# The first layer of a four-layer graph network: program order on three engines, edge sums of two adjacency blocks together, node sums by transposes, an earlier u and later weights

## The chip, the cores and the metric

The kernel runs on one core of one Trainium2 chip. The metric is the device time of one execution in microseconds (us). Every execution also has a mean granted clock of the tensor engine.

PE is the tensor engine, DVE the vector engine, ACT the scalar engine, SP the engine that issues most loads. PEld is PE loading weights.

## The reference, cut to what matters

Four layers follow each other, each a residual and a layer norm around a graph layer on the same 4096 x 4096 adjacency matrix. The change touches only layer 0.

```python
def _L0_gnn_ref(h, node_adj, edge_adj, W, a):      # both matrices are adj
    hw = h @ W
    pos = (node_adj > 0).astype(hw.dtype)
    neg = (node_adj < 0).astype(hw.dtype)
    h_plus, h_minus = pos @ hw, neg @ hw
    a1, a2 = (a[:F_OUT], a[F_OUT:])
    e_plus = leaky_relu((h_plus @ a1 + h_minus @ a2)[:, 0], ALPHA)
    ...
    scores = jnp.where(edge_adj > 0, e_plus[None, :], NEG_INF)
    scores = jnp.where(edge_adj < 0, e_minus[None, :], scores)
    attn = softmax(scores, axis=1)
    return attn * edge_adj @ hw

x = _layernorm(x + _L0_gnn_ref(x, adj, adj, W, a))
...                                                 # three more layers
```

The matrix has no negative entry with these inputs (the kernel checks it and has a slow path for it), so the layer needs two things: for every node the sum of u = hw @ a1 over its edges, from which e follows, and then products of the matrix with hw scaled by exp(e), with their normaliser.

## The kernel before

The matrix is cut into 8 x 8 blocks of 512 x 512, one load of 1 MB each. The **first pass** runs over the eight rows of blocks. In each block DVE makes a mask of the edges, PE sums u over the edges, and ACT looks for negative entries. At the end of row i the sums are copied (the tile `parts`), and e, its exponential and the scaled hw of row i follow. Products with blocks whose hw is already scaled are done at once. Up to two blocks behind the diagonal are kept on the chip and used later; the **second pass** loads the others again.

```python
def masks(a):
    pos = l0w.tile([P, TB, IB], BF16, name="pos", bufs=4)
    nc.vector.tensor_scalar(pos, a, 0.0, None, op0=ALU.is_gt)
    return pos

def edge_sums(pe, pos, j, wgt, first, last):
    for k in range(TB):
        nc.tensor.matmul(pe[32 * k:32 * k + 32, :], wgt[:, j * TB + k, :], pos[:, k, :], start=first, stop=last)

def columns(parts):                       # node sums: four products with two columns
    pc = ps_tr.tile([P, TB, 2], F32, name="ptr")
    for k in range(TB):
        nc.tensor.matmul(pc[:, k, :], parts[:, k * P:(k + 1) * P], sel, start=True, stop=True)
    return pc

for i in range(NB):                       # first pass
    ...
    for n, j in enumerate(order):
        a = chunk(l0k if i < j <= i + 2 else ld, adjT, i, j)            # (shortened)
        pos = masks(a)
        edge_sums(pe, pos, j, both, n == 0, n == NB - 1)
        nc.scalar.activation(junk, a, AF.Relu, scale=-1.0, accum_out=...)
        if n == 1 and rest:
            diagonal(*rest)               # of row i - 1
            if i >= 3:
                above(i - 3, kept.pop(i - 3))
        ...
        while n > 0 and known:
            j, a = known.pop(0)
            product(p, j, a, j == 0, False)
    if i == 4:
        tc.keep_in_program_order(nc.sync.dma_start(x, ...))             # 2 MB
    nc.scalar.copy(parts, pe)
    sums = columns(parts)
    ...                                   # e, Exp, hw scaled, split into three bf16 parts
```

The framework that builds the kernel chooses the order of instructions on each engine itself; the text of the program only says what depends on what.

The softmax here doesn't subtract the row's maximum and nothing guards it: scores larger than these inputs give would overflow.

## Time and profile before

| | kernel before |
|---|---|
| median of 3 runs | 2280.73 us (2279.25 to 2281.05) |
| span of the profiled run | 2278.0 us |
| busy | PE 96%, DVE 52%, ACT 26% |
| sums of rows 0, 3 and 7 complete | 51.1, 123.9, 265.3 us |
| first product of layer 1 | 353.5 us |

A line of the timeline reads: start, duration, engine, source line, operation, what is written from what is read, shapes, number of instructions in a row, and in brackets how long the engine had been idle and who released it. The start of a row in the kernel before (row 5, PE):

```profile
189.49 0.95 PE L341 MATMUL ptr<-sel,parts 128*128 128x2 f32 x8
190.30 1.10 PE L346 MATMUL pacc<-keep,hw 128*128 128x512 f32 x2
191.33 0.40 PE L334 MATMUL pden<-pos,both 128*32 128x512 bf16 x4
192.02 0.40 PE L334 MATMUL pmm<-pos,xp 128*32 128x512 bf16 x4 [0.29 <-DVE pos L328]
193.83 3.70 PE L346 MATMUL pacc<-chunk,hw 128*128 128x512 f32 x8 [1.41 <-DVE hw L411]
```

Each f32 matmul shows as two records, called passes below, so the product with one block, four matmuls, is eight passes. The `x8` at 189.49 are the node sums. While DVE works on e behind them, PE does two passes of a kept block and edge sums, and is idle for 0.29 + 1.41 us. The product behind runs at full clock: eight passes in 3.70 us.

### The profile page before, as it was taken

To read this page: it belongs to the slowest core of one execution; us is meant where nothing else is said; L and a number is where in the kernel's file an instruction comes from. 1 tells how busy PE (TensorE), PEld (TensorE's weight loads), DVE (VectorE), ACT (ScalarE), POOL (GpSimd) and SP (SyncE) were. 2 spreads that over 40 slices of the span, in tenths; PEclk is the share of its full clock that TensorE was granted. 3 is DMA by queue.
4 is the path that set the end of the run, shared out by engine and by line. 5 is a ranking of instruction groups with operands and counts; after the bars stand their busy time and mean duration, and the time that the engine had idled before them with its cause. 6 is when DMAs were issued, how large, how long until landed. Compare 5 with 4: busy or idle time off the path is not lost.

```text
span 2278.0 us, 22715 instructions
## 1 busy us (share of the span) xinstructions
PE 2176.3 (96%) x8552; PEld 843.0 (37%) x8552; DVE 1176.9 (52%) x1709; ACT 593.6 (26%) x1012; POOL 836.9 (37%) x540
## 2 busy tenths in 40 slices
PE   4899999999999999999999999879999999999998
PEld 3333444444444444444443333212222322232233
DVE  4554462000010110000026777779999999999955
ACT  4764200000000000000032222334444443443320
POOL 0000000000000000000004555669999999999930
PEclk9899999999999999999999999999999999999999
DMA  7886658889777677778876556434666666666665
GB/s 279 336 334 232 213 178 273 300 299 302 266 256 242 233 263 242 263 266 271 274 245 230 201 186 220 167 111 149 223 254 241 224 244 243 243 234 238 238 226 203
DMA packets 83608, 549.14 MB, mean 241 GB/s; under 512 B 9376, under 2 KB 15520, under 8 KB 17568
## 3 DMA queue, kind: packets, MB, share of 16 engines
q1 hardware_dynamic: 75200, 542.15, 68.1%
q10 hardware_dynamic: 8288, 5.44, 0.8%
q8 instruction: 69, 1.13, 0.2%
q14 instruction: 51, 0.42, 0.1%
HBM read 545.46 MB, written 2.10 MB: 240 GB/s over the span
## 4 chain that ended last, share of the span: by engine, by line
PE 83%; DVE 10%; issue 3%; ACT 2%; DMA 1%; ACTq 0%; POOL 0%; DVEq 0%; POOLq 0%
PE pacc L514 29%; PE pacc L346 10%; PE den L705 9%; PE pp L769 9%; PE pp L861 8%; PE num L705 7%; DVE tau L688 5%; DVE tau L691 2%; PE pmm L540 2%; PE num L769 1%; PE pden L334 1%; PE num L861 1%; PE px L135 1%; PE ptr L135 1%; ACT a L666 1%
## 5 line engine op out<-in xcount | busy, mean ns | idle before, releaser
L688 DVE SCALAR_TENSOR_TENSOR tau<-D,es,a 128x1024 f32<-128x1024 f32 x512 | 630.7, 1273 | 27.7 <-ACT a L666 27.5
L693 POOL TENSOR_TENSOR tau<-tau,chunk 128x1024 f32<-128x1024 f32 x256 | 609.4, 2380 | 16.7 <-DVE tau L688 15.9
L612 POOL TENSOR_TENSOR x<-x,B2R 128x512 f32<-128x512 f32 x8 | 10.2, 1279 | 1176.3 <-PE px L135 1176.3
L705 PE MATMUL den<-tau,cs 128*32 128x512 f32 x2048 | 357.0, 608 | 30.7 <-DVE tau L688 22.9
L666 ACT ACTIVATE a<-chunk 128x1024 f32<-128x1024 f32 x232 | 238.7, 1029 | 453.3 <-DVE tau L691 387.6
L705 PE MATMUL num<-tau,hc 128*32 128x512 f32 x2048 | 346.5, 600 | 0.6 <-POOL tau L693 0.6
L692 POOL TENSOR_TENSOR tau<-tau,chunk 128x320 f32<-128x320 f32 x256 | 222.8, 870 | 155.6 <-DVE tau L688 106.2
L769 PE MATMUL pp<-chunk,xT 128*128 128x512 f32 x448 | 236.1, 629 | 0.0
L691 DVE TENSOR_TENSOR tau<-tau,a 128x704 f32<-128x704 f32 x256 | 225.4, 881 | 0.0
L514 PE MATMUL pacc<-chunk,t 128*128 128x512 f32 x512 | 223.5, 592 | 0.0
L514 PE MATMUL pacc<-chunk,v 128*128 128x512 f32 x512 | 222.5, 592 | 0.0
L514 PE MATMUL pacc<-chunk,x 128*128 128x512 f32 x512 | 221.9, 592 | 0.0
L861 PE MATMUL pp<-chunk,w 128*128 128x512 f32 x448 | 208.1, 602 | 2.4 <-ACT xT L565 1.6
L346 PE MATMUL pacc<-chunk,hw 128*128 128x512 f32 x408 | 196.7, 622 | 2.3 <-DVE hw L411 2.3
L705 PEld LDWEIGHTS den<-tau,cs 128*32 128x32 f32 x2048 | 57.9, 107 | 270.2 <-DVE tau L688 180.1
L705 PEld LDWEIGHTS num<-tau,hc 128*32 128x32 f32 x2048 | 88.7, 110 | 145.0 <-issue 132.3
L514 PEld LDWEIGHTS pacc<-chunk,v 128*128 128x128 f32 x512 | 97.2, 190 | 122.0 <-issue 122.0
L514 PEld LDWEIGHTS pacc<-chunk,x 128*128 128x128 f32 x512 | 96.4, 190 | 116.7 <-issue 116.7
L514 PEld LDWEIGHTS pacc<-chunk,t 128*128 128x128 f32 x512 | 96.1, 190 | 115.3 <-issue 115.3
L769 PEld LDWEIGHTS pp<-chunk,xT 128*128 128x128 f32 x448 | 71.7, 188 | 158.6 <-issue 144.3
L561 DVE COPY w<-ptr 128x512 f32<-128x512 f32 x8 | 5.5, 691 | 241.5 <-PE ptr L135 241.5
L861 PEld LDWEIGHTS pp<-chunk,w 128*128 128x128 f32 x448 | 80.5, 190 | 115.7 <-issue 111.6
(190 smaller groups left out, 1443.5 us busy)
## 6 DMA issues: line engine op xcount, KB each, us to landing
chunk<-in_adjT SPq DMA_DIRECT2D x386, 1024.0 KB, 4.9
chunk<-in_adj SPq DMA_DIRECT2D x116, 1024.0 KB, 4.9
keep<-in_adjT SPq DMA_DIRECT2D x13, 1024.0 KB, 6.9
xT<-in_xT ACTq DMA_DIRECT2D x8, 256.0 KB, 6.1
out<-o ACTq DMA_DIRECT2D x8, 256.0 KB, 5.1
W1A<-in_w1a ACTq DMA_DIRECT2D x1, 384.0 KB, 5.6
W1B<-in_w1b ACTq DMA_DIRECT2D x1, 384.0 KB, 6.4
W0T<-in_w0gT ACTq DMA_DIRECT2D x1, 64.0 KB, 5.6
```

The source lines that it names most:

```text
L135: nc.tensor.transpose(p[:, k, :], src(k), ident)
L346: nc.tensor.matmul(p, hw[:, j * TB + k, :], a[:, k, :], start=first and k == 0, stop=last and k == TB - 1)
L514: nc.tensor.matmul(p, stationary(c * TB + k), a[:, k, :], start=n == 0 and k == 0, stop=n == NB - 1 and k == TB - 1)
L540: nc.tensor.matmul(ph, W1A[:, k, hh * P:(hh + 1) * P], r, start=k == 0, stop=k == 2)
L666: nc.scalar.activation(ap, a, AF.Copy, accum_out=deg[:, nt, self.mp:self.mp + 1])
L688: nc.vector.scalar_tensor_tensor(tau[:, h, :], self.D[:, h].rearrange("p b i -> p (b i)"), es[:, nt, 2 * self.hp + h:2 * self.hp + h + 1], ap,
L691: nc.vector.tensor_tensor(tau2[:, 0, 0:OWN], tau[:, 0, 0:OWN], ap[:, 0:OWN], ALU.mult)
L692: nc.gpsimd.tensor_tensor(tau2[:, 0, OWN:WB], tau[:, 0, OWN:WB], a[:, OWN:WB], ALU.mult)
L693: nc.gpsimd.tensor_tensor(tau2[:, 1, :], tau[:, 1, :], a, ALU.mult)
L705: nc.tensor.matmul(acc[q:q + 32, :], weights(nt, 2 * self.hp + h, is_den), r[:, h, mb * IB:(mb + 1) * IB], start=nt == 0, stop=nt == NT - 1)
L769: nc.tensor.matmul(p, y[:, (2 * mp + c) * TB + k, :], a[:, k, :], start=c == 0 and k == 0, stop=c == 1 and k == TB - 1)
L861: nc.tensor.matmul(p, w[:, c * TB + k, :], a[:, k, :], start=c == 0 and k == 0, stop=c == NB - 1 and k == TB - 1)
```

## The change

The intent: let PE, DVE and ACT run in an order written by hand, so that edge sums of two blocks stand together (fewer switches between bf16 and f32 on PE), node sums come from transposes and a vector sum instead of products with two columns, u = x @ (W a) is made first so that the masks can start early, and weights of later layers are loaded when they are not in the way. The core of the diff, with cuts marked:

```diff
-    for g in range(NB):
-        nc.scalar.dma_start(xT[:, g * IB:(g + 1) * IB], xT_in[:, g * IB:(g + 1) * IB])
+    for g in range(2):
+        half = slice(g * N // 2, (g + 1) * N // 2)
+        nc.sync.dma_start(xT[:, half], xT_in[:, half])
...                                        (later weights: collected in `loads`)
+            manual.enter_context(tc.manual_schedule(engines={mybir.EngineType.PE, mybir.EngineType.DVE,
+                                                             mybir.EngineType.Activation}))
+            WA = l0.tile([P, 2], F32, name="WA")
...
+                for k in range(NT // 2):
+                    t = half * NT // 2 + k
+                    nc.tensor.matmul(pu[:, k, :], xT[:, t * P:(t + 1) * P], WA, start=True, stop=True)
...
-                pos = l0w.tile([P, TB, IB], BF16, name="pos", bufs=4)
+                pos = l0w.tile([P, TB, IB], BF16, name="pos", bufs=6)
...
-            def columns(parts):
...
+            def column(dst, q, col):
+                nc.vector.tensor_reduce(dst, q.rearrange("p k (g c) -> p k g c", g=4)[:, :, :, 3 * col:3 * col + 3],
+                                        AX.XY, ALU.add)
...
             for i in range(NB):
...
                     pos = masks(a)
-                    edge_sums(pe, pos, j, both, n == 0, n == NB - 1)
+                    sums.append((j, pos))
+                    if j < i:
+                        known.append((j, a))
+                    if n == 0 and diag:
+                        if behind:
+                            product(diag.p, *behind[0], behind[0][0] == 0, False)
+                        scores(i - 1, parts)
+                        for b in behind[1:]:
+                            product(diag.p, *b, False, False)
+                    if n == 2 and i >= 3:
+                        above = Above(i - 3)
...
+                    elif n % 2:
+                        for m, (b, ps) in enumerate(sums):
+                            edge_sums(pe, ps, b, both, n == 1 and m == 0, False)
+                        sums = []
+                        then = (diag if n == 1 else above if n == 3 else None)
+                        if then:
+                            then.sums()
+                            then.products()
+                            ends.append(then.store)
...
+                        while len(known) > int(n == NB - 3):
+                            b = known.pop(0)
+                            product(p, *b, b[0] == 0, False)
+                    if (i, n) == (1, 3):
+                        for t, src in loads:
+                            tc.keep_in_program_order(nc.sync.dma_start(t, src))
...                                        (second pass: blocks in pairs, loaded and masked one pair ahead)
+                then = Above(NB - 3) if n == 1 else Above(NB - 2) if n == 3 else None
+                if n + 1 < len(pairs):
+                    ahead = load(*pairs[n + 1])
+                while ends:
+                    ends.popleft()()
```

`while len(known) > int(n == NB - 3)` is the held-back product: one block's product waits for the start of the next row, so that PE has something to do while `parts` is copied and transposed.

## The prediction

> **What bounds the kernel now.** I read the page first, then the busy time of every engine stretch by stretch, then the timeline of single instructions in the first 360 us, then the waits of the DMA queue. The page's slices say that after a short ramp the tensor engine never rests:
>
> ```profile
> PE   4899999999999999999999999879999999999998
> ...
> DVE  4554462000010110000026777779999999999955
> ACT  4764200000000000000032222334444443443320
> ...
> PEclk9899999999999999999999999999999999999999
> ```
>
> Each digit is 57 us. Only the first slices are under 9 on PE, and only there is the granted clock below 0.9. The change touches the first layer alone. Layer 1 begins with its first product at 353.5 us (first start of the group of line 514 that reads x), so the first layer owns 353 of 2278 us, and everything behind it is moved as a block. What the change is worth is therefore how far that start moves. The same view by engine in five stretches of that layer:
>
> ```profile
> core 0: us, PE busy (x) PEld busy (x) DVE busy (x) ACT busy (x) POOL busy (x), PEclk, DMA share, GB/s
> 0.00:50.00 50.00, 19.69 (x95) 14.87 (x99) 22.06 (x92) 21.68 (x33) 0.70 (x6) 0.99 0.81 303
> 50.00:95.00 45.00, 38.57 (x148) 15.33 (x140) 22.86 (x38) 35.11 (x41) 0.00 (x0) 0.78 0.90 365
> 95.00:124.00 29.00, 26.66 (x95) 10.29 (x96) 14.78 (x23) 17.55 (x21) 0.00 (x0) 0.88 0.69 266
> 124.00:265.00 141.00, 139.05 (x478) 56.10 (x481) 62.39 (x94) 70.54 (x80) 0.00 (x0) 1.00 0.73 253
> 265.00:353.00 88.00, 88.00 (x346) 41.98 (x339) 54.72 (x173) 8.44 (x17) 0.00 (x0) 1.00 0.58 197
> ```
>
> I cut at 95, 124 and 265 because there the sums of rows 2, 3 and 7 of the adjacency matrix are complete (the copies of `parts` at 94.9, 123.9 and some 265.5; rows 0 and 1 end at 51.1 and 70.2). So there are two regimes. Up to 124 us the engine waits: for data (365 GB/s, DMA 0.90), for the small chain at the end of each row, and at a low clock (0.78). From 124 us on it is PE work end to end: 139 of 141 us and 88 of 88. A change helps the first part by shorter waiting, and the second only by less PE work.
>
> The unit of that work can be read from the timeline of PE in row 6:
>
> ```profile
> 208.50 0.40 PE L334 MATMUL pden<-pos,both 128*32 128x512 bf16 x4
> 208.83 3.70 PE L346 MATMUL pacc<-chunk,hw 128*128 128x512 f32 x8
> 212.46 0.40 PE L334 MATMUL pden<-pos,both 128*32 128x512 bf16 x4
> ```
>
> One block of 512x512: four bf16 edge matmuls, then four f32 products as eight passes, every 3.96 us. The passes follow each other every 0.43 us, so a product block is 3.43 us; the rest, 0.53, is the edge group with its switch. Elsewhere twelve edge matmuls together took 0.76 us and four took 0.33 until the product began: each further group costs 0.21, so a group is 0.21 and a switch between the kinds 0.32.
>
> **What the Trainium skill says.** "TensorE: Matmul & The Clock Gate", Part 1 (The HAM clock gate), has the array fall to half clock after about 3.4 us with little to do and come back after as long a busy stretch. The trace agrees: after a gap at 96.6 to 98.4 us four product passes took 3.78 us, against eight in 3.70 later. The same page, Part 3 (Packing small matmuls), says matmuls to different column groups run at once; the four edge matmuls in 0.40 us show that. "DMA: Bandwidth & Descriptors", section Issuing engines are not separate DMA queues, says that loads issued from several engines share the same 16 DMA engines, so moving a load to another queue changes order, not bandwidth. The DMA share of 0.9 to 1.0 between 10 and 30 us, with both queues active, agrees.
>
> **The change, part by part.**
>
> *Start.* Now, eight loads of xT and nine small weights stand on ACT's queue; ACT's first copy starts at 18.6 us behind the load of ATS, and the eight chunks of products x@W, each waiting for ACT's copies, stretch to 47 us, because `both` for a block comes from the same matmuls. Changed, u (two columns) is made first: 64 passes, of 0.107 us warm or 0.234 us cold by the node-sum group, 7 to 15 us from 9.7 us on. So all of u is split by some 20 to 26 us. Then masks come at 1.13 us each. But ACT still has eight passes of 2.03 us over the chunks and eight copies of 0.58, and can't do its third before the first x@W, some 5 us after u: 26 to 32 + 12.2 + 3.5 + 0.6, so `parts` at about 40 to 45 instead of 51.1. Gain 6 to 11 us.
>
> *Rows 1 to 3.* In each, e and Exp come first (4 us after `parts`), then ACT's eight passes (16.2) with the stores, and the later chunks' buffers are freed by these passes. I get about 20 us for row 1 (now 19), 22 for row 2 (now 24.7) and 28.5 for row 3, which PE fills with six blocks (now 29). Row 3 then ends at 111 to 117 instead of 123.9. I take 112.
>
> *Rows 4 to 7 and the second pass.* 54 blocks remain: 185.2 us. 63 edge groups at 0.21: 13.2. Two blocks together make 25 switches (four a row, nine in the second pass) at 0.32: 8.0. Node sums of e: five transposes of four with a switch, 3.0. Finishing: eight blocks with three transposes of four at 0.5: 12.0. Sum 221 us. Now it is 229.5 us from 123.9 to 353.4, with fewer blocks left over, since a few of line 346 lie before it. So transposes in place of the matmuls with 128 weights and two columns (eight passes 0.80 to 0.95, a transpose of four 0.50) save 13 x 0.35 = 4.5 us; pairing saves less than it looks, some 3 us, since the scheduler already put groups together at row ends.
>
> *What program order adds.* At the start of a row PE does one held-back product (3.6 us, hides the copy of `parts`), then the transposes, and then waits: the vector engine has the whole chain of e, Exp, hw scaled (0.69) and the split (six at 0.2), some 3.0 us, and the mask of the second block (1.13) behind it. PE's next pair needs that mask. Rows 4, 5 and 6 hold back one block only, so each has a hole of about 3.9 us; rows 7 and the second pass hold two and hide it. Now the scheduler filled such places with other products (1.7 us idle at 192, none at 225). 3 x 3.9 = 11.7; for the clock falling in them I take 3 us in all; some 2 to 3 us in the second pass for adds behind masks. Sum 17.
>
> *Later weights* leave the first 20 us free for chunks, but their 0.4 MB is one us of transfer: nothing by itself.
>
> Layer 1 would begin at 112 + 221 + 17 = 350, against 353.5: the time falls by 3 us, to 2278.
>
> **Rivals.** (a) The row-start hole is filled or cheap, because the chain on the vector engine is shorter than I think, and the ramp reaches the transfer limit: 34 MB at 0.4 MB/us ends row 3 at about 95 to 100. Then layer 1 begins at 325 to 335 and the time is 2252 to 2262. For it: the author wrote the held-back products on purpose; DMA does run at 428 GB/s around 85 us. Against it: buffers are freed by ACT, at 2.03 us a chunk with the exp chain in between. (b) A new wait takes the place of the old: every hole lets the clock fall to half for a window (the 96 us gap cost about 2 us besides its own length), six rows have it, and u runs cold. Then row 3 ends at 120, the rest takes 244, and the time is 2290. For it: the trace shows exactly this at 98 us after a gap shorter than mine. Against it: at 125 and 192 us gaps of the same chain left the clock at full. (c) PE's work stays the bound and the order doesn't matter at all: only the 7 us of work saved show, 2273. (d) The vector engine becomes the bound: no, it is busy 62 of 141 us.
>
> **Range and chances.** To be faster by over 2% the change must save 46 us; all the time PE does not work in the first 124 us is about 39 us, and data must still arrive, so that is very unlikely. To be slower by 2% it would have to lose 46 us in a layer whose work falls; the holes together can't. So within 2% at 0.95. Predicted 2278 us; the rivals span 2252 to 2290, and a little beyond on the high side, so 2256 to 2294.
>
> **What would show it.** In the changed kernel: `parts` of row 0 at 40 to 45 us and of row 3 near 112; a hole of 3 to 4 us on PE, ended by a mask, at each start of rows 1 to 6, and none at row 7; product passes at twice 0.43 us behind some of them; a first product of layer 1 near 350 us; and everything from there on the same length as now, 1924 us. If row 3 ends at 100 or the holes are absent, rival (a) holds; if the clock column stays below 0.9 to 250 us, rival (b). The prediction is wrong if the layers behind change, for example because the first chunks of layer 1 or its weights arrive later than now.

## The result, and the profile after

| | before | after |
|---|---|---|
| median of 4 runs | 2280.89 us (2279.25 to 2281.45) | 2295.28 us (2292.88 to 2296.17) |
| span of the profiled run | 2278.0 us | 2293.8 us |
| sums of row 0 complete | 51.1 | 43.7 |
| sums of row 3 complete | 123.9 | 120.5 |
| sums of row 7 complete | 265.3 | 269.6 |
| first product of layer 1 | 353.5 | 368.8 |
| from there to the end | 1924.5 | 1925.0 |

The ratio is 1.0063, with a 95% interval of 1.0045 to 1.008. A ratio here is the mean time of one kernel's runs over the mean of the other's runs of the same rounds, so it isn't quite the ratio of the medians quoted. The time lies 1 us above the predicted range.

The slices of the page of the kernel after:

```profile
PE   6789989999999999999999999979999999999998
...
PEclk9899999999999999999999999989999999999999
```

The first slice holds more PE work than before (6 for 4), but the third and sixth (115 to 172 and 287 to 344 us) are no longer full (8 for 9). The busy time of every engine in five stretches, cut at the ends of rows as in the prediction (the columns are span, busy time with number of instructions of PE, PEld, DVE, ACT and POOL, then granted clock, share of the DMA engines, GB/s):

```profile
0.00:50.00 50.00, 28.68 (x170) 24.77 (x171) 16.92 (x38) 24.22 (x30) 0.70 (x6) 0.97 0.78 303
50.00:88.00 38.00, 26.92 (x107) 10.44 (x107) 22.08 (x41) 29.82 (x35) 0.00 (x0) 0.81 0.96 382
88.00:120.00 32.00, 27.11 (x94) 11.27 (x97) 14.99 (x29) 17.24 (x20) 0.00 (x0) 0.90 0.76 267
120.00:270.00 150.00, 137.35 (x465) 57.21 (x458) 61.06 (x93) 70.62 (x81) 0.00 (x0) 0.95 0.67 232
270.00:368.00 98.00, 90.72 (x319) 41.24 (x318) 61.41 (x181) 9.36 (x18) 0.00 (x0) 0.97 0.56 192
```

Rows 4 to 7 (120 to 270) had 139 busy of 141 us at clock 1.00; now they have 137 of 150 at 0.95. The second pass had 88 of 88 at 1.00; now 91 of 98 at 0.97. PE idles 20 us there, and runs slower behind.

What an idle stretch looks like, from the timeline of PE at the start of row 5:

```profile
160.93 0.60 PE L140 MATMUL ptr<-ident,parts 128*128 128x128 f32 x4
161.46 0.40 PE L338 MATMUL pden<-pos,both 128*32 128x512 bf16 x4
165.43 0.40 PE L338 MATMUL pden<-pos,both 128*32 128x512 bf16 x4 [3.57 <-DVE pos L332]
165.65 0.40 PE L338 MATMUL pden<-pos,xp 128*32 128x512 bf16 x4
165.98 12.26 PE L348 MATMUL pacc<-chunk,hw 128*128 128x512 f32 x24
```

and what DVE does in the same time:

```profile
161.57 0.21 DVE L343 TENSOR_REDUCE e<-ptr 128x4 f32<-128x48 f32 x1 [5.04 <-PE ptr L140]
...
162.45 0.69 DVE L360 TENSOR_TENSOR hw<-hw,xe 128x512 f32<-128x512 f32 x1 [0.27 <-ACT xe L359]
...
164.08 0.18 DVE L362 COPY both<-xp 128x12 bf16<-128x12 bf16 x1
164.16 2.35 DVE L332 TENSOR_SCALAR pos<-chunk 128x2048 bf16<-128x2048 f32 x2
```

PE has done the edge sums of the row's first block and wants those of the second, whose mask is the first half of the DVE instruction at 164.16. In program order that mask stands behind the whole chain of e, 2.6 us from 161.57 on. DVE was idle for 5.04 us before that chain: it isn't slow, it stands in the wrong place. Behind the hole 24 product passes take 12.26 us; in row 7, which has no hole, 24 take 10.57. So the hole costs 3.57 us and 1.7 more.

The longest hole is in the second pass. PE at 310 us, and DVE in the same stretch:

```profile
310.64 0.62 PE L338 MATMUL pden<-pos,xp 128*32 128x512 bf16 x8
317.33 0.62 PE L338 MATMUL pmm<-pos,xp 128*32 128x512 bf16 x4 [6.07 <-DVE pos L332]
317.88 6.29 PE L348 MATMUL pmm<-keep,hw 128*128 128x512 f32 x8
```

```profile
310.09 0.21 DVE L343 TENSOR_REDUCE z<-ptr 128x4 f32<-128x48 f32 x1
...
315.02 1.11 DVE L155 TENSOR_SCALAR x<-x,mv,rstd 128x128 f32<-128x128 f32 x4
316.05 1.22 DVE L332 TENSOR_SCALAR pos<-keep 128x2048 bf16<-128x2048 f32 x1
```

The mask of the kept block stands behind a complete finishing chain of another row of blocks (310.09 to 316.1). Eight passes behind take 6.29 us instead of 3.70.

### The profile page after: what moved, and what is told of

Read it like the earlier page. It is cut to its first block, busy times and chain, and to the rows that moved or that the text cites. A ratio compares the mean times of both kernels' runs of the same rounds, so it can differ in the third digit from the quotient of the medians.

```text
span 2293.8 us, 22626 instructions
## 1 busy us (share of the span) xinstructions
PE 2177.3 (95%) x8552; PEld 851.5 (37%) x8552; DVE 1177.0 (51%) x1670; ACT 592.0 (26%) x1004; POOL 836.9 (36%) x540
## 4 chain that ended last, share of the span: by engine, by line
PE 81%; DVE 11%; issue 3%; ACT 3%; DMA 2%; POOL 0%; DVEq 0%; ACTq 0%; SPq 0%; POOLq 0%
PE pacc L603 29%; PE den L794 9%; PE pp L858 9%; PE pp L950 8%; PE num L794 7%; PE pacc L348 6%; DVE tau L777 5%; DVE tau L780 2%; PE pmm L348 2%; PE pmm L629 2%; PE num L858 1%; PE num L950 1%; DVE pos L332 1%; PE ptr L140 1%; PE px L140 1%
```

## The experiments

Theory: program order is what costs the time. It puts a mask that PE needs behind a chain on DVE that PE doesn't need, and the clock falls in the hole. Rivals: the order of blocks or the transposes make PE's work longer; the late copies of xT and the start take the time; or the transfers are the limit and holes only show it. Each run below is of five rounds with the kernel before on the same chip, all gave correct results, and all were within 2%, so the intervals matter. The kernel before itself ran between 2271 and 2285 us over these sessions; differences of less than about 0.3% are therefore read from profiles, and only with care.

One try did not build: a fourth buffer for kept blocks needs 64 KB in each partition, and 49.8 KB were left. So the buffers of kept blocks could not be taken away as a limit in that way.

### Program order taken away

```diff
-            manual.enter_context(tc.manual_schedule(engines={mybir.EngineType.PE, mybir.EngineType.DVE,
-                                                             mybir.EngineType.Activation}))
```

> The changed kernel with the fixed program order taken off (the scheduler orders tensor, vector and scalar engine again); everything else of the change stays. Theory A (the loss is what program order does: holes at the starts of rows with a cold clock behind them, and one 6 us hole in the second pass): the holes go, the 7 us of saved work and the quicker start show, 2268 to 2278 us, first product of layer 1 at 341 to 351 us. Rival B (u first, or paired sums, or loading, cost the time whatever the order): stays at 2290 to 2297 us, layer 1 at 364 to 369.

2266.29 us, ratio 0.9953 (0.9936 to 0.997), a little better than expected. Nothing else was touched, so all other parts of the change are in it. Layer 1 begins at 339.0 us instead of 368.8. The start of row 5 there, on PE:

```profile
184.01 0.60 PE L140 MATMUL ptr<-ident,parts 128*128 128x128 f32 x4
184.54 0.62 PE L336 MATMUL pden<-pos,both 128*32 128x512 bf16 x8
185.09 6.28 PE L346 MATMUL pacc<-chunk,hw 128*128 128x512 f32 x14
```

PE has its masks already and goes on without a pause. Because this was the largest effect, both kernels were run once more in one session.

> The changed kernel itself on the same chip as its version without program order: ratio 1.005 to 1.008, so 1.0 to 1.5% above auto_again.

> The changed kernel without program order once more, for comparison on this chip: ratio 0.992 to 0.996.

With program order 2295.72 us (1.007, 1.0053 to 1.0087), without it 2266.78 us (0.9949, 0.9933 to 0.9966): the difference is 28.9 us, and layer 1 begins at 369.6 and 340.1 us. The waits of PE behind row 3 (line, releaser: us in total, times, longest), first with program order, up to 270 us and from there, then without it, up to 252 us:

```profile
PE pden L338 <- DVE pos L332: 11.9, 5, 3.6
```

```profile
PE pmm L338 <- DVE pos L332: 6.1, 1, 6.1
```

```profile
PE pacc L346 <- DVE hw L358: 0.8, 1, 0.8
```

Without program order PE waits 0.8 us in all, and its granted clock from there to layer 1 is 1.00. The loss is program order, and the rest of the change is a small gain; as the same blocks are loaded in both, the transfers were not the limit.

### Held-back products and an earlier mask

If the hole at a row's start is the limit, a second product held back in rows 2 to 5 must fill the holes of rows 3 to 6.

```diff
-                        while len(known) > int(n == NB - 3):
+                        while len(known) > ((n == 3) + 2 * (n == 5) if 2 <= i <= 5 else int(n == NB - 3)):
```

> The changed kernel with two products held back instead of one at the ends of rows 2 to 5, so that the second runs on the tensor engine while the vector engine makes e and the masks. Theory A: the holes of 3.57 us at 94, 126, 163 and 200 us and the 1.7 us of half clock behind each go, up to 21 us in the row lengths; as row 3 is partly short of data, 14 to 21 us: 2274 to 2281 us, row 7's parts at 249 to 256 us (now 269.6). Rival B (the holes only move: held chunks keep buffers and the next loads come later, or the row is bound by data): under 6 us.

2289.91 us, 1.0058 (1.004 to 1.0075); layer 1 at 367.8 us, so a gain of 1 us where 14 to 21 were expected. The holes at row starts are gone. But row 4 takes 35.5 us, as before the edit (35.3), since PE now waits at the row's end. PE, DVE and SP in row 4 of this run, each from its timeline:

```profile
148.72 0.40 PE L338 MATMUL pden<-pos,both 128*32 128x512 bf16 x4
151.27 0.40 PE L338 MATMUL pden<-pos,both 128*32 128x512 bf16 x4 [2.15 <-DVE pos L332]
153.82 0.59 PE L338 MATMUL pden<-pos,both 128*32 128x512 bf16 x4 [2.15 <-DVE pos L332]
```

```profile
149.99 1.23 DVE L332 TENSOR_SCALAR pos<-keep 128x2048 bf16<-128x2048 f32 x1 [3.91 <-DMA keep<-in_adjT]
```

```profile
141.95 3.76 SPq L133 DMA_DIRECT2D keep<-in_adjT  x2
```

PE waits for a mask, the mask for a load of a kept block, and that load was issued at 141.95 us because its buffer was in use until then: the products of the blocks kept three rows earlier free it, and they come late in the row (the waits of SP between 120 and 160 us list 8.1 us for them). In the kernel after the same load is issued at 142.36 us. The buffer is not all of it: in both runs the load of x was issued 7.5 us before the kept block (134.45 and 134.85 us) and was still under way until 147.5 and 147.9 us, and the kept block took 8.0 us to land, against 4.8 us in row 3. So a second limit of nearly the same length lies under the hole, the late arrival of the kept blocks, to which the buffers and the load of x both add. The prediction's picture, in which the hole alone sets the row, fell here.

In the second pass, the mask of the kept block was made one pair earlier.

```diff
+            late = {}
             for n, (i, js) in enumerate(pairs):
                 now = ahead
-                then = Above(NB - 3) if n == 1 else Above(NB - 2) if n == 3 else None
+                late = {1: Above(NB - 3)} if n == 1 else {3: Above(NB - 2)} if n == 2 else late
+                then = late.pop(n, None)
```

> The changed kernel with the mask of the last kept block of the second pass made one step earlier, ahead of a finishing chain on the vector engine. Theory A: the hole of 6.07 us at 311 us and the 2.6 us of half clock behind it go, less 1.1 us for a later add: 6 to 8.7 us, 2286.5 to 2289.5 us. Rival B (the vector chain comes due there anyway and another wait takes its place): 0 to 2 us.

2287.52 us, 1.0048 (1.003 to 1.0066), within what was expected. The hole of 6.07 us is gone; what is left of it on PE:

```profile
303.47 0.60 PE L140 MATMUL ptr<-ident,x 128*128 128x128 f32 x4
305.96 0.66 PE L140 MATMUL ptr<-ident,xT 128*128 128x128 f32 x4 [1.89 <-DVE xT L384]
...
308.36 4.96 PE L348 MATMUL pmm<-keep,hw 128*128 128x512 f32 x8
```

Layer 1 begins at 358.0 us, 10.8 us earlier in the profile. Of this, 4.6 us are there at the end of row 7 already, most of it from row 5 (35.0 for 38.4 us), which the edit doesn't touch; 6.2 us belong to the second pass and so to the mask. By the ratios (1.0048, against 1.0063 and 1.007 for the kernel after in other sessions) it is 3 to 5 us.

Both edits together:

> Both mends in one kernel. If they are independent the gains add: 20 to 30 us, 2265 to 2275 us, which is below the kernel before (2281). If they share a cause (the vector engine's order) less than the larger of the two.

2286.49 us, 1.004 (1.0023 to 1.0057); layer 1 at 357.4 us, far from the 2265 to 2275 us expected. That is the mask's gain alone, so the second held-back product is worth nothing here either.

### The kept blocks used earlier

If the kept buffers set the second limit, using the blocks earlier in the row frees them earlier. The masks of these blocks are made at the row's first block, and their sums and products follow those of the diagonal.

```diff
+                    if n == 0 and i >= 3:
+                        above = Above(i - 3)
                     if n == 0 and diag:
...
-                    if n == 2 and i >= 3:
-                        above = Above(i - 3)
...
-                        then = (diag if n == 1 else above if n == 3 else None)
-                        if then:
-                            then.sums()
-                            then.products()
-                            ends.append(then.store)
+                        now = [then for then in (diag, above) if then and n == 1]
+                        for then in now:
+                            then.sums()
+                        for then in now:
+                            then.products()
+                            ends.append(then.store)
```

> The changed kernel with the kept blocks of row i-3 taken at the start of the row (their masks before the e chain, sums and products straight after the diagonal block) and one product held back as in the change. They free the two kept buffers some 8 to 14 us earlier, for which the loads of the row's next kept blocks and of all chunks behind them in the queue wait. Theory C (rows 4 to 6 have two limits of nearly the same length: the tensor engine with its hole, and the loads that wait for the kept buffers): alone it does little, as the holes of 3.57 us with 1.7 us of cold clock stay; 0 to 6 us under the changed kernel, ratio to before 1.0035 to 1.006. Rival D (only the loads set the row length): 15 us or more under it, ratio under 1.0.

2294.72 us, 1.0076 (1.0058 to 1.0094); layer 1 at 366.1 us. Alone it gives nothing, since the hole at the row's start (3.58 us at row 5) is still there. With the second held-back product as well:

> The same with two products held back in rows 2 to 5. Theory C: both limits go, rows 4 to 7 take 130 to 136 us (149 in the changed kernel), 12 to 19 us under the changed kernel, ratio to before 0.998 to 1.001. Rival D: no better than the one before. Rival E (the hold-back keeps five chunk buffers so full that loads come late anyway): under 6 us.

2286.71 us, 1.0033 (1.0016 to 1.005), short of the 0.998 to 1.001 expected; layer 1 at 360.6 us. Row 4 falls from 35.3 to 28.1 us. Alone, each edit left the time where it was within a few us; both together took 7 us from row 4, and 8 us from the time of the run with the earlier blocks alone. So the hole and the late kept blocks were two limits of one length. How much of the second was buffers isn't shown: here the kept loads were issued at 134.91 and 138.34 us, ahead of the load of x (138.88), and landed in 4.8 us; with the earlier blocks alone the first one was issued at 138.68 us, 3.7 us earlier than in the kernel after, but behind x, and landed only 0.5 us earlier (149.9 for 150.4). The edit freed buffers and took x out of the way at once. But row 5 rises from 38.4 to 41.2 us. PE, DVE and SP at the start of row 5:

```profile
155.92 0.40 PE L338 MATMUL pden<-pos,both 128*32 128x512 bf16 x4 [1.52 <-DVE pos L332]
161.91 0.62 PE L338 MATMUL pden<-pos,both 128*32 128x512 bf16 x4 [5.60 <-DVE pos L332]
```

```profile
154.64 1.23 DVE L332 TENSOR_SCALAR pos<-chunk 128x2048 bf16<-128x2048 f32 x1 [9.04 <-DMA chunk<-in_adjT]
```

```profile
138.88 0.85 SPq L477 DMA_DIRECT2D x<-in_x  x1
141.83 27.83 SPq L133 DMA_DIRECT2D chunk<-in_adjT  x5
```

The load of x (2 MB), now moved behind row 4's blocks, is a third limit: it is issued between the loads of rows 4 and 5 and takes 13.2 us from issue to landing; the row's first block is issued behind it, and DVE waits 9.04 us for that block. With the earlier mask of the second pass added:

> The same with the mask of the second pass made a step earlier too: another 6 to 8 us under the one before, ratio to before 0.994 to 0.998, so like the changed kernel without program order (0.9953). If theory C holds, program order is not slow as such: it lost by what stands in the order.

2279.67 us, 1.0005 (0.9988 to 1.0022), where 0.994 to 0.998 was expected; layer 1 at 354.5 us. Three small edits of the order bring the program-ordered kernel back to the time of the kernel before.

### The load of x

```diff
-                if i == 4:
+                if i == 6:
                     tc.keep_in_program_order(nc.sync.dma_start(x, ...))
```

> above_first_all with the load of x put behind row 6 instead of row 4. If x's load ahead of row 5's chunks is what is left: row 5 falls from 41 us to 31 to 34, 7 to 10 us off the whole, ratio to before 0.996 to 0.9975 (above_first_all 1.0005). If row 5's chunks wait for full buffers anyway: under 3 us.

2278.64 us, 1.0005 (0.9989 to 1.0021), no gain where 7 to 10 us were expected. Row 5 falls from 41 to 31.5 us, but row 7 takes 46.6 us instead of about 38.7. The hole has moved with the load; PE at the start of row 7:

```profile
227.02 0.62 PE L338 MATMUL pden<-pos,both 128*32 128x512 bf16 x4 [5.59 <-DVE pos L332]
```

So the load of x is the cause, and in both places tried, in one piece ahead of a row's first block, it costs as much. (Without program order the same load is issued at 130.58 us and takes 12.4 us, and PE waits only 0.8 us in all behind row 3: the other order has work ready. Whether its size or its pieces of 512 bytes make the load slow, no run tells.) In four pieces, after rows 4 to 7:

```diff
-                if i == 4:
-                    tc.keep_in_program_order(nc.sync.dma_start(x, ...))
+                if i >= 4:
+                    q = slice((i - 4) * NT // 4, (i - 3) * NT // 4)
+                    tc.keep_in_program_order(nc.sync.dma_start(x[:, q, :], ...[:, q, :]))
```

> above_first_all with the load of x in four quarters, one behind each of rows 4 to 7 (3 us each instead of 13 at once). If x's load is the last wait in the rows: rows 4 to 7 take 129 to 134 us (143 in above_first_all, 141 with x behind row 6), layer 1 at 342 to 348 us, ratio to before 0.994 to 0.9975. If a quarter before each row is as bad, as every row's first chunks then come late: no better than 1.0005.

2273.46 us (five runs), 0.9982 (0.9966 to 0.9999); layer 1 at 349.2 us. Rows 4 to 7 take 138.5 us where 129 to 134 were expected, a partial miss. In this run PE waits only 5.0 us between the end of row 3 and layer 1, and yet takes 231.6 us for that stretch, against 218.7 without program order. Of these 12.9 us, 4.2 are waiting (5.0 against 0.8). The product passes counted in the stretch are 440 against 426, which at 0.43 us is 6.0 us of work that the other order had done before row 3 ended. The remaining 2.7 us can come from the clock (0.98 against 1.00), which I have not separated further.

### The parts of the change without program order

Starting from the kernel without program order, each part was undone. First the node sums, by products with two columns again:

```diff
-                q = transpose4(ps_tr, "ptr", lambda k: pe[:, k * P:(k + 1) * P])
-                column(e[:, tb], q, 0)
-                column(den[:, tb], q, 1)
+                q = columns(pe)
+                nc.vector.tensor_copy(e[:, tb], q[:, :, 0])
+                nc.vector.tensor_copy(den[:, tb], q[:, :, 1])
...                                        (the same in finish)
```

> The changed kernel without program order, node sums made as before, by matmuls with 128 weights and two columns (eight passes 0.80 to 0.95 us) instead of transposes (0.50 us for four): some 13 of the 16 lie in the dense part, 13 x 0.35 = 4.5 us slower, ratio to before 0.9973 (without program order 0.9953). If they lie beside other work: no change.

2268.53 us, 0.9947 (0.993 to 0.9964), by time no change; layer 1 at 344.7 us, 5.7 us later than with transposes in the profile. Behind row 3, PE spends 6.7 + 4.9 us on 96 passes with two columns, where it spends 4.2 + 3.1 us on 48 transposes: 4.3 us.

Then the edge sums, one block at a time:

```diff
-                    sums.append((j, pos))
+                    edge_sums(pe, pos, j, both, n == 0, n == NB - 1)
...
-            pairs = [(i, list(range(j, min(j + 2, NB)))) for i in range(NB - 3) for j in range(i + 3, NB, 2)]
+            pairs = [(i, [j]) for i in range(NB - 3) for j in range(i + 3, NB)]
```

> The changed kernel without program order, edge sums block by block as before. By the switch of 0.32 us per group saved: at most 25 to 30 switches in the dense part, 3 to 9 us slower, ratio 0.9965 to 0.999. If the scheduler puts groups together anyway: under 2 us.

2267.95 us, 0.994 (0.9924 to 0.9956), by time no change; layer 1 at 345.0 us, 6.0 us later in the profile. But 4.3 us of these are there at the end of row 0 (50.6 for 46.3), and they aren't the edge groups': the second 32 passes of u, ahead of any edge sum, take 6.83 us in this run and 3.71 in the first one with pairs (more on this in the last section). From the end of row 3 to layer 1 it takes 220.1 us, against 217.4 and 218.7 in the two runs with pairs, so pairs are worth 1.4 to 2.7 us there.

Then the start (eight loads of xT and all weights on ACT's queue, u and x @ W from the same products, later constants at once; a long diff that restores the lines shown with a minus above):

> The changed kernel without program order, with the start as before: x and all small weights on the scalar engine's queue at once, u from the same matmuls as x@W. Row 0's parts return to 51 us and row 3's to 124 (now 46.3 and 121.5): 3 to 6 us slower, ratio 0.9965 to 0.998. If the start's lead is given back by row 3: no change.

2260.68 us, 0.9913 (0.9892 to 0.9934); layer 1 at 338.0 us, 1 us earlier than with the new start. Row 0 ends later (49.3 instead of 46.3 us), and row 3 doesn't (120.1 instead of 121.5): the lead of the early u is given back by row 3. All three undone together:

> The changed kernel without program order and with node sums, edge groups and start as before; only the order in which the blocks are programmed stays changed. Sum of the three by the profiles (5.7 + 6.0 - 1.0 us in layer 1's start): 8 to 14 us slower than auto_again, ratio to before 0.999 to 1.001. Rival: the gain lies in the order of the blocks, ratio 0.993 to 0.996.

2273.54 us, 0.9979 (0.9962 to 0.9996); layer 1 at 345.3 us, against 340.1 in the same session. The time lies between the two expectations. By time alone the runs with columns and with single groups can't be told apart from the kernel without program order; the one with the old start (0.9892 to 0.9934) lies at or under it (0.9936 to 0.997 and 0.9933 to 0.9966), so the new start gains nothing. Read from row 3 to layer 1, where every profile has full clock, the parts add up: columns make that stretch 4.3 to 5.6 us longer (223.0), single groups 1.4 to 2.7, all three undone 5.8 to 7.1 (224.5). Each is one profile, and the two runs to compare with differ by 1.3 us. What this leaves to the new order of the program's text, and to six mask buffers instead of four, is the 0.2% by which this run still beats the kernel before.

### The best version

Row 0 of the kernel without program order is held by ACT: PE waits 9.07 us for ACT's copy of `parts` in the second such run. The eight copies of x @ W were therefore moved to DVE.

```diff
-                nc.scalar.copy(hw[:, g * TB:(g + 1) * TB, :], pn)
+                nc.vector.tensor_copy(hw[:, g * TB:(g + 1) * TB, :], pn)
```

> The changed kernel without program order, with the eight copies of x@W in row 0 made by the vector engine instead of the scalar one, which is the busy one there (8 passes of 2.03 us and 8 copies of 0.58 us; parts of row 0 at 46.3 us). If the scalar engine limits row 0: parts at 41 to 43 us and 3 to 5 us off the whole, ratio to before 0.993 to 0.9945. If the loads or the chain of the next rows do: under 1 us, 0.995.

2262.03 us, 0.9927 (0.991 to 0.9944). Row 0 ends at 42.6 instead of 46.3 us, and 3 us of that are still there at layer 1 (335.8). With the start as before in addition:

> No program order, the start as before, and the copies of x@W made by the vector engine: paired sums, transposes and the order of blocks are what stays of the change. If the start's two gains add: parts of row 0 at 45 us, layer 1 at 333 to 337, 2257 to 2262 us, ratio 0.990 to 0.993. If the vector engine's copies now hold up its masks: 0.994 or more.

2260.49 us, 0.9923 (0.9906 to 0.994); layer 1 at 334.2 us. This beats both kernels, by about 0.8% and, by the ratios, 1.4% (0.9923 against 1.0063). In the profile PE is busy in the whole of the stretch from 117 us to layer 1, at clock 1.00. It can't be told by time from the two runs before it with the same or the old start (2260.68 and 2262.03).

## Why the prediction was right or wrong

**Right: the place and the frame.** Only the first layer moved; behind it 1925.0 us against 1924.5. "Within 2%" came out, and so did the reasons why neither side of 2% could be reached. The tensor engine's work was sized right: the prediction has 221 us from row 3 to layer 1, and the kernel after takes 248.3 us there, of which 19.7 are waits (12.5 + 7.2) and 9.1 a low clock (4.8 behind the holes of rows 4 to 6, 1.7 behind two short waits at the end of row 4, where eight passes at 155.69 us took 5.40, and 2.6 in the second pass). That leaves 219.5.

**Right: the mechanism.** The hole of 3 to 4 us, ended by a mask, is there in rows 1 to 6 (4.88 us in row 1, 3.57 in the others), absent in row 7, and followed by slower passes. The kernel without program order shows that the fixed order makes these waits; that filling the row holes alone gained 1 us shows that they weren't the only limit.

**Wrong: the step "What program order adds", in size.** Its sum was 17 us; it measured 28.8. Term by term:

| term | predicted | measured |
|---|---|---|
| holes at the starts of rows 4 to 6 | 11.7 | 10.7 |
| further waits for masks in rows 4 to 7 | 0 | 1.8 |
| clock | 3 | 9.1 |
| waits in the second pass | 2 to 3 | 7.2 |

The prediction had the hole about right and mis-sized what comes with it. "For the clock falling in them I take 3 us in all" came to 1.4 to 1.7 us behind each hole, 1.7 behind the short waits and 2.6 behind the hole in the second pass. It looked at the kernel before, where gaps at 125 and 192 us left the clock at full, and took these as a sign against rival (b); but the gap at 192 us was 0.29 + 1.41 us, less than half of what it was predicting. In the second pass it priced only adds, and overlooked that a mask of a kept block, made late in the program, stands behind a finishing chain of 6 us.

**Wrong: row 3.** "I take 112" against 120.5. The prediction's own chain of rows sums to 43.7 + 20 + 22 + 28.5 = 114 with the measured row 0; the rows took 20.9, 23.1 and 32.8. Row 3 is six blocks at 3.96 us, 23.8, as it said, and then its own hole of 3.6, two groups of passes at low clock (2 x 1.7), the products of the later constants (0.9) and a wait of 1.3. The prediction named holes for rows 1 to 6 and put only those of rows 4 to 6 into its sum.

Put together: 112 + 8.5 for row 3, and behind it 221 - 1.5 for work and 17 + 11.8 for program order, give the 368.8 measured. The nearest rival was (b), with 2290 and row 3 at 120; it named the slower passes. Its remainder of 244 us was still 4 short, by the second pass.

**Right in number, partly by luck: row 0**, 43.7 in a range of 40 to 45. The prediction's own sum, 26 to 32 + 12.2 + 3.5 + 0.6, gives 42.3 to 48.3. The reason given for u held: its 64 passes took 13.8 us, the long end of 7 to 15. **A misreading without effect:** PE is under 9 not only in the first slices of the page before; slices 26, 27 and 40 read 8, 7 and 8, all behind layer 0. **Not tested alone: later weights.** The run with the old start, which loads them early again, shows no loss. **Borne out by profiles, not by time: the gain of single parts.** The 4.5 us for transposes are met by 4.3 us of PE time in the profile. Pairs were put at 3 us and gave 1.4 to 2.7 behind row 3 without program order.

**What the prediction could not have shown**, and the runs did: under the hole lay more limits, the late kept blocks and the load of x. A reader of the profile after, seeing 3.57 us holes ended by DVE, would fill them and gain nothing.

## What to carry to other kernels

If you fix the order of instructions by hand, look for every short wait of the critical engine at what stands in front of its releaser in that engine's order: here a mask of 1.2 us stood behind chains of 2.6 and 6 us that nobody on PE needed. Price such a hole with the clock behind it, and before filling it, look which loads were issued late in the same stretch, since a buffer freed late or one large load in front may be a limit of the same length. And run a hand-made order once against the automatic one with everything else equal; here that single run showed the whole loss.

## What the Trainium skill lacked or had wrong

- "TensorE: Matmul & The Clock Gate", section Why this matters for your kernels, advises "No PE-idle gaps >~3µs between matmul bursts". The holes of 3.57 us agree, with 1.4 to 1.7 us lost behind each. But shorter gaps cost clock too in places where only transposes or edge sums stood around them: behind a gap of 1.89 us in the second pass eight passes took 4.96 us, and in row 2 of the kernel after, behind a gap of 2.25 us, 5.40 instead of 3.70. In these two the stretch without a large product was 4.9 and 3.4 us long. The section doesn't say that small matmuls may fail to keep the clock up; of transposes the page's Part 4 says so, but I found nothing on edge sums of this size.
- Same page, Part 1 (The HAM clock gate): it has full clock after about 3.4 us of sustained work. The 64 passes of u, each with two columns behind a weight load of 128 x 128, kept 0.216 us a pass for all of their 13.8 us. Without program order 32 such passes took 6.99 us, and the next 32, behind products with 128 columns, 3.71 us (0.116 a pass). The granted clock of the profile reads 1.00 in both stretches, but the first entry of the clock record in the trace, at full clock, stands at 33.0 us in the kernel after and at 20.5 us without program order, just where the passes get short; in the run with single edge groups it stands at 33.3 us, and the same second 32 passes took 6.83 us. A clock of 1.00 ahead of the first entry is therefore not to be trusted, and in the kernel after 13.8 us of such narrow passes did not bring the clock up.
- "DMA: Bandwidth & Descriptors", Queues, rings and completion order, says that the descriptors of a ring are consumed in order. I found no page that says what it costs when the issuing engine waits for a buffer or has one large load in front: a load of 2 MB took 13.2 us to land and made the vector engine wait 9.04 us for the block issued behind it, and a kept block issued at 142 us behind it, when its buffer came free, took 8.0 us to land instead of 4.8.
- I found no page on an order by hand against the framework's own: it was 28.9 us of 2296 in one session.
